# Cross-attention on one core: a new order table, scores with single banks, exponentials emitted bank by bank

## The chip, the core and the metric

The kernel runs on one core of a Trainium2 chip, in one launch. All data is fp32. The metric is the device time of that core in microseconds (us). Before the change the median of three runs is 495.86 us (495.84 to 495.98).

## The reference: what is computed

Tokens x (2 batches of 2048, width 640) attend to a context of 154 rows (width 1024) in 20 heads of 32. The first 77 context rows are text, the other 77 image prompts; each set has its own keys, values and softmax, and the two results are added. An output projection with bias follows, and x is added as residual:

```
q = heads(x @ Wq.T)
out = softmax(q k_text.T / sqrt(32)) v_text + softmax(q k_ip.T / sqrt(32)) v_ip
y = merge(out) @ Wo.T + bo + x
```

## The kernel before

Matrices come laid out with the contracted dimension first. The 640 channels are 5 chunks c of 128 (4 heads each), and a product q = 5 b + c names batch and chunk (0 to 9). Its 2048 tokens are two units u = 2 q and 2 q + 1 of 1024 tokens, each in two blocks h of 512. The 8 row tiles (128 tokens) of a unit fall into three groups s: 3, 3 and 2 tiles. Names are made of these numbers: `R1.12` is group 1 of unit 12.

For each group the work is a chain over four engines:

- `q.u.h` (line 206): TensorE projects 512 tokens into one PSUM bank, ten matmuls in the profile (each program matmul stands there as two). `cq` (line 220) is its scaled copy by ACT.
- `R` (line 242): scores of 4 heads, on 32-row tiles of the array, into four banks, one for each head. A group has 12 or 8 program matmuls (24 or 16 in the profile).
- `K` (line 254): ACT copies the four banks to `pb` in SBUF. `M` (line 290): VectorE takes maxima. `S` (line 304): POOL subtracts them. `E` (line 310): ACT's exponential. `D` (line 315): VectorE's sums; `I` (line 320): their reciprocals. `N` (line 325): POOL multiplies. `T` (line 332): VectorE transposes.
- Three sets name the groups that go another way. `DIRECT`: no K and no S; maxima are read out of the banks (line 293), and the exponential reads the banks with the maximum as bias, one activation for every row set of 77 (line 278). `BIASED`: K as usual, no S, the same small activations out of `pb`. `SUMMED`: the small activations also accumulate the sums, each with a read of the accumulator, and D falls away.
- `A.q` (line 341): the attention product of two units, 160 matmuls on 32x32 tiles, into four banks; `CA` (lines 364, 368) copies them out. It needs every `T` of both units, and the squares of v that `VS` (line 160) moves by 16 small transfers.

`k` and `v` (line 144) project the context, `ck` and `cv` copy it out. `m`, `o`, `p`, `z` (lines 480, 499, 509) are output products; batch 0 uses seven instead of eight products on halves, with sums `G` (POOL) of rows and `W` of weights and results taken by `cm` and `co` (VectorE). Batch 1 uses a scheme of 33 products `F` (line 887), with weight sums `V` (lines 864, 866) and sums of attention rows `X` (line 872), taken by `Y` (lines 827, 830). `X.B.p` is the first of these row sums; `.d` is VectorE and `.p` POOL.

Transfers go through SyncE's queue: `LK` loads weights of k and v, `LQ` of q, `LX` blocks of x for batch 1, `LO` the output weight, `SF` the residual, and `SS` stores.

What sets the order is a hand-fed table: `SCHEDULE` is one string of words, and `emit` issues each word's instructions. Every engine, and SyncE's queue, runs its own instructions strictly in the order of the table; waits come from the data, the buffers and the banks. `@` names the bank, or for R and A the half of PSUM: banks 0 to 3 or 4 to 7. In the rows of the order below, bank_67 to bank_74 are banks 0 to 7. Ahead of the table stands a fixed opening (the first projections and loads), which the change leaves as it is.

Of the kernel before, what the change touches and what calls it, by code (L numbers as in the profile page):

```python
# [9 lines left out]
F32 = mybir.dt.float32  # L10
AF = mybir.ActivationFunctionType
# [9 lines left out]
def kernel(  # L21
# [43 lines left out]
        (11, 0), (12, 0), (13, 0), (13, 2), (14, 0), (14, 2), (15, 1), (15, 2), (18, 1), (19, 2),  # L65
    }
    BIASED = {
        (2, 2), (3, 2), (4, 2), (6, 2), (8, 2), (9, 2), (11, 2), (12, 1), (16, 2), (17, 2), (18, 2),
    }
    SUMMED = {  # L70
        (4, 2), (11, 2), (12, 0), (13, 0), (13, 2), (14, 0), (15, 1), (15, 2), (16, 2), (17, 2), (18, 1),
        (18, 2), (19, 2),
# [13 lines left out]
    halves = banks[:G], banks[G:]  # L86
# [145 lines left out]
    def rows_of(u, s):  # L232
        return keys_of(u, s).rearrange("p n g (t l) -> p (n g) t l", l=L)
# [36 lines left out]
    def exponential_of(u, s, ps=None, den=None):  # L270

        n = GROUPS[s][1]
        for g in range(G):
            for t in range(n):
                for x in range(2):
                    row = rows_of(u, s)[:, t * G + g, x]
                    one = t * G + g, slice(x, x + 1)
                    nc.scalar.activation(  # L278
                        row,
                        row if ps is None else rows_in(ps[g], n)[:, t, x],  # L280
                        AF.Exp,
                        bias=maxs[(u, s)][:, *one],
                        accum_out=None if den is None else den[:, *one],
                    )
# [300 lines left out]
    for t in range(2):  # L585

        ps = halves[t][G - 2 + t]
        project_kv(t, ps)
        for b in range(B):
            nc.scalar.copy(kT[:, 0, b, t, :], keys_in(ps)[:, b])  # L590
# [345 lines left out]
```

## Time and profile before

| what | value |
|---|---|
| median of the runs | 495.86 us |
| span of the profiled execution | 494.6 us |
| TensorE busy | 489.1 us, 99% |
| VectorE busy | 413.9 us, 84% |
| POOL busy | 370.5 us, 75% |
| ACT busy | 309.5 us, 63% |
| granted TensorE clock | 1.00 throughout |
| HBM read and written | 54.94 and 10.49 MB |

The profile is of one execution; its own time is the span, from the first to the last instruction, and the median of the runs is 1.3 us above it. The chain of waits is followed back from the last instruction and lists each stretch with start, length, engine and line; the groups list busy time and mean length for each line and form; the timeline has the instructions in order of time with the idle time before them and what ended it. Matmul ends are modelled, so the distance from one start to the next says more than a matmul's own length.

### The profile page before, as it was taken

To read this page: it belongs to the slowest core of one execution; us is meant where nothing else is said; L and a number is where in the kernel's file an instruction comes from. 1 tells how busy PE (TensorE), PEld (TensorE's weight loads), DVE (VectorE), ACT (ScalarE), POOL (GpSimd) and SP (SyncE) were. 2 spreads that over 40 slices of the span, in tenths; PEclk is the share of its full clock that TensorE was granted. 3 is DMA by queue.
4 is the path that set the end of the run, shared out by engine and by line. 5 is a ranking of instruction groups with operands and counts; after the bars stand their busy time and mean duration, and the time that the engine had idled before them with its cause. 6 is when DMAs were issued, how large, how long until landed. Compare 5 with 4: busy or idle time off the path is not lost.

```text
span 494.6 us, 10484 instructions
## 1 busy us (share of the span) xinstructions
PE 489.1 (99%) x4116; PEld 287.7 (58%) x4116; DVE 413.9 (84%) x416; ACT 309.5 (63%) x1002; POOL 370.5 (75%) x158
## 2 busy tenths in 40 slices
PE   9999999999999999999999999999999999999997
PEld 5666648558557556456566654754755675444443
DVE  0069989989899989979988896687789898999996
ACT  1275788977687778677899786587889862100000
POOL 0069988988988988879886758475689899798700
PEclk9999999999999999999999999999999999999999
DMA  8992046203241724895540666455550212320125
GB/s 278 350 288 80 17 124 181 67 1 95 62 150 44 247 65 146 270 345 178 161 172 27 215 195 223 134 172 183 184 169 19 90 42 85 129 85 2 42 85 212
DMA packets 67105, 69.38 MB, mean 140 GB/s; under 512 B 5488, under 2 KB 47088, under 8 KB 67056
## 3 DMA queue, kind: packets, MB, share of 16 engines
q1 hardware_dynamic: 66048, 67.54, 43.7%
q10 hardware_dynamic: 1008, 1.18, 0.7%
q8 instruction: 32, 0.52, 0.4%
q14 instruction: 17, 0.14, 0.1%
HBM read 54.94 MB, written 10.49 MB: 132 GB/s over the span
## 4 chain that ended last, share of the span: by engine, by line
PE 96%; DMA 3%; ACTq 0%; ACT 0%; DVE 0%; DVEq 0%; issue 0%
PE bank L206 34%; PE bank L887 12%; PE bank L341 11%; PE bank L242 11%; PE bank L499 10%; PE bank L144 9%; PE bank L480 7%; PE bank L509 3%; DMA aT<-in_L_xattn_Wk_ip_dram 2%; DMA x<-in_x_dram 1%; ACTq L538 0%; ACT pb L254 0%; ACTq L552 0%; DVE acc L830 0%; DVEq L931 0%
## 5 line engine op out<-in xcount | busy, mean ns | idle before, releaser
L325 POOL TENSOR_TENSOR pb<-pb,rden 128x1848 f32<-128x1848 f32 (+1 forms) x60 | 176.0, 2943 | 30.4 <-DVE rden L320 23.6
L304 POOL TENSOR_TENSOR pb<-pb,mx 128x1848 f32<-128x1848 f32 (+1 forms) x39 | 121.6, 3129 | 55.4 <-DVE mx L290 55.3
L206 PE MATMUL bank<-x,wq 128*128 128x512 f32 x280 | 125.4, 598 | 0.1
L332 DVE STREAM_TRANSPOSE pb<-pb 128x1920 f32<-128x1920 f32 (+1 forms) x60 | 115.9, 1938 | 9.1 <-POOL pb L325 8.9
L290 DVE TENSOR_REDUCE mx<-pb 128x24 f32<-128x1848 f32 (+1 forms) x50 | 91.6, 1844 | 32.1 <-ACT pb L254 31.9
L254 ACT COPY pb<-bank 128x462 f32<-128x462 f32 (+1 forms) x200 | 85.3, 542 | 29.3 <-PE bank L242 28.9
L315 DVE TENSOR_REDUCE den<-pb 128x24 f32<-128x1848 f32 (+1 forms) x47 | 88.9, 1895 | 15.6 <-ACT pb L310 12.8
L206 PEld LDWEIGHTS bank<-x,wq 128*128 128x128 f32 x280 | 51.7, 190 | 60.0 <-issue 58.8
L310 ACT ACTIVATE pb<-pb 128x1848 f32<-128x1848 f32 (+1 forms) x39 | 65.6, 1684 | 17.5 <-POOL pb L304 17.4
L278 ACT ACTIVATE pb<-bank,mx 128x77 f32<-128x77 f32 x208 | 60.4, 387 | 6.5 <-DVE mx L293 6.5
L278 ACT ACTIVATE pb<-pb,mx 128x77 f32<-128x77 f32 x184 | 54.1, 356 | 1.9 <-DVE mx L290 1.8
L341 PE MATMUL bank<-pb,v 32*32 32x512 f32 x1600 | 55.2, 597 | 0.0
L206 PE MATMUL bank<-x,aT 128*128 128x512 f32 x116 | 51.8, 596 | 0.0
L242 PEld LDWEIGHTS bank<-kT,qT 32*128 32x128 f32 x1024 | 36.1, 184 | 21.6 <-issue 13.3
L144 PE MATMUL bank<-wo_ct,aT 128*128 128x154 f32 x320 | 46.0, 297 | 0.7 <-DMA aT<-in_L_xattn_Wk_ip_dram 0.4
L144 PEld LDWEIGHTS bank<-wo_ct,aT 128*128 128x128 f32 x320 | 43.0, 188 | 4.7 <-issue 3.0
L242 PE MATMUL bank<-kT,qT 32*128 32x154 f32 x1024 | 45.1, 305 | 0.0
L278 ACT ACTIVATION_READ_ACCUMULATOR pb<-bank,mx 128x1 f32 x168 | 44.0, 266 | 0.0
L341 PEld LDWEIGHTS bank<-pb,v 32*32 32x32 f32 x1600 | 29.0, 103 | 22.7 <-issue 10.1
L480 PE MATMUL bank<-aT,wo_ct 128*128 128x512 f32 x80 | 36.3, 595 | 0.0
L206 PEld LDWEIGHTS bank<-x,aT 128*128 128x128 f32 x116 | 21.4, 190 | 23.7 <-issue 23.5
L220 ACT ACTIVATE qT<-bank 128x512 f32<-128x512 f32 x32 | 19.3, 631 | 23.4 <-PE bank L206 23.4
(83 smaller groups left out, 524.2 us busy)
## 6 DMA issues: line engine op xcount, KB each, us to landing
x<-in_x_dram SPq DMA_DIRECT2D x20, 1280.0 KB, 6.7
out_dram<-acc SPq DMA_DIRECT2D x19, 256.0 KB, 2.9
x<-in_x_dram SPq DMA_DIRECT2D x17, 256.0 KB, 5.9
acc<-in_x_dram SPq DMA_DIRECT2D x16, 256.0 KB, 4.4
out_dram<-x SPq DMA_DIRECT2D x15, 256.0 KB, 2.0
v<-vS SPq DMA_DIRECT2D x160, 20.0 KB, 2.7
aT<-in_L_xattn_Wk_dram SPq DMA_DIRECT2D x5, 512.0 KB, 6.0
aT<-in_L_xattn_Wk_ip_dram SPq DMA_DIRECT2D x5, 512.0 KB, 5.5
```

The costliest lines, as they stand in the source:

```text
L144: nc.tensor.matmul(keys_in(out), loaded[n][:, k, :], cT[:, k, :, t, :], start=(k == 0), stop=(k == NCC - 1))
L206: nc.tensor.matmul(pq, weight_of(q)[:, k, :], xs[place_of(u, h)][:, k, :], start=(k == 0), stop=(k == NC - 1), skip_group_check=loose,)
L242: nc.tensor.matmul(ps[g][:, ts(t, 2 * L)], qTs[(u, h)][g * D : (g + 1) * D, ts(st, P)], kT[g * D : (g + 1) * D, c, b].rearrange("p t l -> ...
L254: nc.scalar.copy(keys_of(u, s)[:, :, g], ps[g][:, : n * 2 * L].rearrange("p (n l) -> p n l", n=n))
L278: nc.scalar.activation(row, row if ps is None else rows_in(ps[g], n)[:, t, x], AF.Exp, bias=maxs[(u, s)][:, *one], accum_out=None if den i ...
L290: nc.vector.tensor_reduce(mx, rows_of(u, s), AX.X, ALU.max, negate=negate)
L304: nc.gpsimd.tensor_tensor(rows_of(u, s), rows_of(u, s), maxs[(u, s)].unsqueeze(3).to_broadcast([P, n, 2, L]), ALU.subtract)
L315: nc.vector.tensor_reduce(den_of(u, s), rows_of(u, s), AX.X, ALU.add)
L325: nc.gpsimd.tensor_tensor(rows_of(u, s), rows_of(u, s), rdens[(u, s)].unsqueeze(3).to_broadcast([P, n, 2, L]), ALU.mult)
L332: nc.vector.transpose(p, p)
L341: nc.tensor.matmul(pa[r][g * D : (g + 1) * D, :], v4s[q % 2][rows, g, k, :], zones[rows, :, g, k, :], start=(k == 0), stop=(k == NK - 1),)
L480: nc.tensor.matmul(ps, wo[:, k, ts(NC - 1, P)], rows_of_attention(b, k)[:, i], start=(k == 0), stop=(k == NC - 1),)
```

## The change

1. The table has new words from its start up to the first sum of attention rows (`X.B.p`); behind it the words are nearly the same, with a few neighbours swapped and other bank numbers.
2. R and A no longer take a half of PSUM. The table names four banks, in the order in which the four heads (for A the four row groups) use them.
3. The exponential of a small-activation group is emitted in four words, one for each bank: `E0.1.0` to `E0.1.3`. A group with one big activation still runs it at the first of the four; the other three do nothing.
4. The three sets change: 10 to 8 groups DIRECT, 11 to 13 BIASED, 13 to 16 SUMMED.

The computation is otherwise the same. The diff, with two lines of the table for many:

```diff
     DIRECT = {
-        (11, 0), (12, 0), (13, 0), (13, 2), (14, 0), (14, 2), (15, 1), (15, 2), (18, 1), (19, 2),
+        (1, 2), (9, 1), (11, 0), (13, 0), (13, 2), (15, 1), (18, 1), (19, 2),
     }
     BIASED = {
-        (2, 2), (3, 2), (4, 2), (6, 2), (8, 2), (9, 2), (11, 2), (12, 1), (16, 2), (17, 2), (18, 2),
+        (2, 2), (4, 2), (5, 2), (6, 2), (8, 2), (11, 2), (12, 1), (13, 1), (15, 2), (16, 2), (17, 2), (18, 2),
+        (19, 1),
     }
     SUMMED = {
-        (4, 2), (11, 2), (12, 0), (13, 0), (13, 2), (14, 0), (15, 1), (15, 2), (16, 2), (17, 2), (18, 1),
-        (18, 2), (19, 2),
+        (1, 2), (2, 2), (4, 2), (5, 2), (6, 2), (8, 2), (11, 2), (12, 1), (13, 1), (15, 1), (15, 2), (16, 2),
+        (17, 2), (18, 1), (18, 2), (19, 2),
     }
...
-    halves = banks[:G], banks[G:]
...
-    def exponential_of(u, s, ps=None, den=None):
+    def exponential_of(u, s, g, ps=None, den=None):
         n = GROUPS[s][1]
-        for g in range(G):
-            for t in range(n):
-                for x in range(2):
+        for t in range(n):
+            for x in range(2):
...
-        "A.4@1 K1.10 M2.10 S0.10 M1.10 S2.10 E0.10 q.12.1@1 CA.4 D0.10 S1.10 E2.10 D2.10 R0.11@1 cq.12.1 E1.10 "
...
+        "K0.10 q.12.0@2 T2.9 T1.9 G5.0 LX.12.1 LX.13.0 VS.5.1 cq.12.0 R1.10@1460 M2.10 K1.10 A.4@3752 M0.10 S2.10 "
+        "M1.10 R0.11@1460 CA.4 q.12.1@3 M0.11 W0 S0.10 E2.10.0 LQ.7 E0.11.0 LX.14.0 VS.6.0 E0.11.1 W1 m2.0@2 "
...
         if k[0] == "R":
-            at[name] = halves[int(where)]
+            at[name] = [banks[int(n)] for n in where]
             scores(x, i, at[name])
         elif k == "A":
-            at[name] = halves[int(where)]
+            at[name] = [banks[int(n)] for n in where]
             attend(x, at[name])
...
                 elif direct or biased:
-                    exponential_of(
-                        x, i, ps if direct else None, den_of(x, i) if (x, i) in SUMMED else None
-                    )
-                else:
+                    if (x, i) in SUMMED and (x, i) not in dens:
+                        den_of(x, i)
+                    exponential_of(x, i, int(args[1]), ps if direct else None, dens.get((x, i)))
+                elif args[1] == "0":
                     exponential(x, i)
```

The places that the prediction speaks of follow, as rows of one engine in program order (line, operation, what it writes and reads, size; line numbers of the changed kernel are one lower from the output sums on). A line of dots leaves out rows of the same run.

TensorE at unit 4, groups 2 and 0 (R2.4 and R0.4) behind the projection q.5.0, before:

```order
L206 MATMUL bank_73<-x_84,aT 128x512 x5
L242 MATMUL bank_67<-kT,aT 128x154
...
L242 MATMUL bank_70<-kT,aT 128x154
L242 MATMUL bank_71<-kT,aT 128x154
L242 MATMUL bank_72<-kT,aT 128x154
L242 MATMUL bank_73<-kT,aT 128x154
...
L144 MATMUL bank_67<-wo_ct,aT 128x154 x8
```

And now:

```order
L206 MATMUL bank_69<-x_84,aT 128x512 x5
L242 MATMUL bank_70<-kT,aT 128x154
...
L242 MATMUL bank_68<-kT,aT 128x154
L144 MATMUL bank_72<-wo_ct,aT 128x154 x8
L242 MATMUL bank_69<-kT,aT 128x154
...
L242 MATMUL bank_72<-kT,aT 128x154
L206 MATMUL bank_69<-x_85,aT 128x512 x5
```

Before, the second group's third bank (73) is the one that the projection had just written; now its bank (69) comes first in a run that the context projection v.2.0 (L144) precedes, and groups 0 and 1 of unit 4 follow each other.

TensorE at unit 12, before (R1.12, q.13.0, the output product m1.0, R0.12):

```order
L242 MATMUL bank_67<-kT,qT_1_1957 128x154
...
L242 MATMUL bank_70<-kT,qT_1_1957 128x154
L206 MATMUL bank_74<-x_82,wq_75 128x512 x5
L499 MATMUL bank_73<-aT,wo_ct 128x256 x4
L242 MATMUL bank_67<-kT,qT_0_1827 128x154
...
L242 MATMUL bank_70<-kT,qT_0_1827 128x154
L206 MATMUL bank_72<-x_83,wq_76 128x512 x5
```

And now (o.0, R0.12, R1.12, m1.0, q.13.0):

```order
L479 MATMUL bank_68<-aT,wo_ct 128x512 x5
L242 MATMUL bank_74<-kT,qT_0_1838 128x154
...
L242 MATMUL bank_68<-kT,qT_1_2004 128x154
L498 MATMUL bank_74<-aT,wo_ct 128x256 x4
L206 MATMUL bank_69<-x_82,wq_75 128x512 x5
```

The two score groups of unit 12 were parted by a projection and an output product; now they are one run, and its last bank (68) is the one that o.0 wrote just ahead of it.

SyncE's queue around the output weight (L166), ahead of A.4, before:

```order
L160 DMA v_0_80<-vS_0_93 32x160 x8
L468 DMA res<-in_x_dram 128x512
L188 DMA x_83<-in_x_dram 128x5x512
L194 DMA wq_75<-in_L_xattn_Wq_dram 128x5x128
L160 DMA v_0_80<-vS_0_93 32x160 x8
L188 DMA x_84<-in_x_dram 128x5x512
L166 DMA wo_ct<-in_L_xattn_Wo_dram 128x5x640
```

And now:

```order
L160 DMA v_0_80<-vS_0_93 32x160 x8
L194 DMA wq_75<-in_L_xattn_Wq_dram 128x5x128
L188 DMA x_83<-in_x_dram 128x5x512
L166 DMA wo_ct<-in_L_xattn_Wo_dram 128x5x640
L160 DMA v_0_80<-vS_0_93 32x160 x8
L188 DMA x_84<-in_x_dram 128x5x512
```

The output weight moved ahead of the last eight v transfers (VS.4.1) and of the block for q.12.1 (x_84); the fetch into `res` moved far ahead.

More of the change, by code (lines that the diff above doesn't have):

```diff
@@ L268, in den_of @@
         return dens[(u, s)]
-    def exponential_of(u, s, ps=None, den=None):
+    def exponential_of(u, s, g, ps=None, den=None):
         n = GROUPS[s][1]
-        for g in range(G):
-            for t in range(n):
-                for x in range(2):
[L276 to L283, printed above, removed]
-                    )
+        for t in range(n):
+            for x in range(2):
+                row = rows_of(u, s)[:, t * G + g, x]
+                one = t * G + g, slice(x, x + 1)
+                nc.scalar.activation(
+                    row,
+                    row if ps is None else rows_in(ps[g], n)[:, t, x],
+                    AF.Exp,
+                    bias=maxs[(u, s)][:, *one],
+                    accum_out=None if den is None else den[:, *one],
+                )
     def maxima(u, s, ps=None, negate=False):
@@ L585 @@
     for t in range(2):
-        ps = halves[t][G - 2 + t]
+        ps = banks[G * t + G - 2 + t]
         project_kv(t, ps)
@@ L701, in emit @@
                 elif direct or biased:
-                    exponential_of(
-                        x, i, ps if direct else None, den_of(x, i) if (x, i) in SUMMED else None
-                    )
-                else:
+                    if (x, i) in SUMMED and (x, i) not in dens:
+                        den_of(x, i)
+                    exponential_of(x, i, int(args[1]), ps if direct else None, dens.get((x, i)))
+                elif args[1] == "0":
                     exponential(x, i)
```

140 rows, old and new, of the table SCHEDULE are left out of this document.

## The prediction, on record before the result

> **What bounds the kernel now.** I read the page first, then the chain of waits in order of time, then busy time by stretch, then groups by form. From the page, the span, the busy time of each engine, the granted clock and the make-up of the chain that ended last:
>
> ```profile
> span 494.6 us, 10484 instructions
> PE 489.1 (99%) x4116; PEld 287.7 (58%) x4116; DVE 413.9 (84%) x416; ACT 309.5 (63%) x1002; POOL 370.5 (75%) x158
> PEclk9999999999999999999999999999999999999999
> PE 96%; DMA 3%; ACTq 0%; ACT 0%; DVE 0%; DVEq 0%; issue 0%
> ```
>
> TensorE is busy 99% of the span at full clock, and 96% of the last chain is TensorE. So an order can win only what TensorE loses between pieces of work. A busy share does not show this, because matmul ends are modelled; the chain does. Its rows are start, length, engine and line, matmuls joined (each program matmul stands as two):
>
> ```profile
> 39.38 1.78 PE bank L242 x48
> 96.01 4.29 PE bank L206 x10
> 100.30 1.00 PE bank L242 x24
> 101.30 4.49 PE bank L206 x10
> 105.79 5.45 PE bank L341 x154
> 111.24 1.00 PE bank L242 x24
> 116.65 1.52 PE bank L242 x40
> ```
>
> L242 is a score run (word R), L206 a projection of queries (q), L341 an attention product (A). First, score runs of 24, 40 and 48 matmuls take 1.00, 1.52 and 1.78: 0.0325 per matmul and 0.22 for the run however long it is, also right behind an A (111.24). Two R words back to back pay the 0.22 once. Second, the same ten matmuls of L206 take 4.29 behind another full-array piece and 4.49 behind R: coming back from the small tiles of R or A to the full array costs 0.20. I call R and A words with nothing else between them a tile stretch.
>
> Third, real waits. A pair of R words (x40) should take 1.52. In this fence stand all the pairs that took longer, with what followed where the wait spilled over:
>
> ```profile
> 91.96 1.74 PE bank L242 x38
> 129.06 1.74 PE bank L242 x38
> 166.16 1.75 PE bank L242 x40
> 203.34 1.03 PE bank L242 x24
> 204.38 0.53 ACT pb L254
> 204.95 4.56 PE bank L206 x10
> 228.53 1.67 PE bank L242 x39
> 273.35 1.76 PE bank L242 x40
> ```
>
> The excess is 0.22, 0.22, 0.23, 0.16 (203.34 to 204.95 is 1.61, or 0.09, and 4.56 against 4.49 another 0.07), 0.18 (228.53 to the next piece at 230.23 is 1.70) and 0.24: 1.25 us together. All have one cause: the pair needs the banks of one half in fixed order, and one of them was written 0.6 to 1.0 us before by a q, o or m word that ACT or DVE has not yet read out.
>
> **The change part by part.**
>
> *Form changes.* Read off the TensorE words of the two tables, the tile stretches ahead of and with A.9 fall from 50 to 46 and the score runs in them from 46 to 44. Up to A.4 both counts are equal (22 and 22 ahead of it); the gain lies between A.4 and A.9. Saved: 4 x 0.20 + 2 x 0.22 = 1.24 us. TensorE's work itself is the same, matmul for matmul, so nothing else changes in its sum.
>
> The Trainium skill's page "TensorE: Matmul & The Clock Gate", section "Part 3: Packing small matmuls — row/col tiling", says that weight loads overlap running matmuls only when the row groups differ. By it full-array loads would lie open everywhere, the return from tiles would cost nothing extra, and this term would be 0.44. The rows disagree: the return costs 0.20 in each row shown. I go by the rows.
>
> *Bank waits.* Every R and A word now names its four banks one by one. The bank freed last is put last in its run, or a short projection stands between. Where the order shows q.5.0 on bank 69, v.2.0 now stands between the two score words and R0.4 has 2.9 us instead of 0.69 until it needs that bank, so the 0.22 at 91.96 is gone; likewise at 129.06. In other places the bank need stays short. By the words and the lengths above: R0.8 needs the bank of q.9.0, and R0.10 that of q.11.0, 0.72 us after it (0.69 cost 0.22 before, so about 0.19 each). o.0 and o.1 take the first bank of an R word with only one short R (0.63 us) between. Such a first copy ends some 0.8 us after its run: 0.17 each. R1.12 needs o.0's bank and R2.11 that of m2.0 0.98 us after them, as the rows at 228.53 and 273.35 did (0.18 and 0.24) where VectorE reads the bank; it may be free in time, so I take half, 0.10 each. Sum 0.92, from 0 (all hidden) to 1.25 (no better than before). Saved: 1.25 - 0.92 = 0.33.
>
> *Work on the other engines.* The three sets that choose how a group of attention rows is computed change. Forms and mean lengths in ns, from the groups by form:
>
> ```profile
> L315 DVE TENSOR_REDUCE den<-pb 128x16 f32<-128x1232 f32 x12 | 17.0, 1416 | 3.8 <-ACT pb L310 2.2 <-ACT pb L278 1.5
> L290 DVE TENSOR_REDUCE mx<-pb 128x16 f32<-128x1232 f32 x16 | 22.5, 1409 | 2.8 <-ACT pb L254 2.6
> L293 DVE TENSOR_REDUCE mx<-bank 128x4 f32<-128x308 f32 x16 | 6.5, 469 | 1.1 <-PE bank L242 1.1
> L304 POOL TENSOR_TENSOR pb<-pb,mx 128x1848 f32<-128x1848 f32 x33 | 108.3, 3289 | 54.5 <-DVE mx L290 54.5
> L278 ACT ACTIVATION_READ_ACCUMULATOR pb<-pb,mx 128x1 f32 x80 | 16.1, 202 | 0.0
> ```
>
> Ahead of A.4, five more small groups sum on ACT: VectorE loses 5 x 1.42 = 7.1 us of sums and gains under 1 us for two groups that reduce out of banks (four of 0.47 for one of 1.41 in the small one). ACT pays 5 x 16 accumulator reads of 0.20 = 16 us at most; they partly run under the next activation, so 8 to 16. POOL does one subtraction of 3.29 less. How much room there is:
>
> ```profile
> 27.00:210.00 183.00, 182.91 (x1793) 112.23 (x1795) 170.51 (x129) 139.41 (x324) 163.24 (x55) 1.00 0.42 120
> 140.22 2.17 DVE L332 STREAM_TRANSPOSE pb<-pb 128x1920 f32<-128x1920 f32 x1
> 142.88 5.45 PE bank L341 x150
> ```
>
> The first row (27 to 210 us) has TensorE, weight loads, DVE, ACT and POOL. VectorE is busy 170.5 of 183, and its last transpose for A.2 ends at 142.39, 0.49 ahead of A.2. So VectorE is the engine that could stop TensorE, and the change takes 6 us from it just there; ACT goes from 139 to at most 155 of 183. All this is hidden beside TensorE and I cost it at 0. Without that cover, a late transpose is paid one to one at the next A. A summed group is now emitted a bank at a time, in four pieces, so that copies on ACT's queue, and then TensorE, wait behind 4 or 6 activations at most, not 16 or 24.
>
> *The tail.* From the first sum of rows on, order and work are nearly the same. It must start earlier, or it swallows the gain. The links closest to TensorE:
>
> ```profile
> 417.77 2.18 DVE L332 STREAM_TRANSPOSE pb<-pb 128x1920 f32<-128x1920 f32 x1 [0.36 <-POOL pb L325]
> 427.41 1.48 DVE L872 TENSOR_TENSOR pb<-aT 128x1024 f32<-128x1024 f32 x1 [0.36 <-PE bank L341]
> 440.60 1.37 POOL L866 TENSOR_TENSOR pb<-wo_ct,pb 128x128 f32<-128x128 f32 x1 [1.19 <-DVE pb L866]
> 441.93 0.45 POOL L866 TENSOR_TENSOR pb<-pb,wo_ct 128x128 f32<-128x128 f32 x1
> 442.85 1.88 PE L887 MATMUL bank<-aT,pb 128*128 128x512 f32 x4
> ```
>
> The weight sum that ends at 442.38 is used at 442.85, 0.47 later. Its chain starts behind A.9 with VectorE's row sum at 427.41, ahead of which VectorE idles 0.36. It moves with A.9 if the last transpose (417.77) is earlier too. That hangs on POOL, which drops the subtraction of unit 19's middle group, 3.29 us, just there. So I cost the tail at 0; bounds 0 and 0.8 (below).
>
> Sum: 1.24 + 0.33 = 1.57 us. The profiled span is 494.6 and the median 495.86, so 1.3 us lie around the span and stay. 495.86 - 1.57 = **494.3 us**. A measurement here tells a change from none at about 0.2%, or 1.0 us.
>
> **The rivals.**
>
> *Swallowed (chance 0.22).* If the last transpose does not move, the row sum at 427.41 starts only 0.36 earlier and the use at 442.85 can come 0.36 + 0.47 = 0.83 earlier: 495.0, no change to be told. New waits of 0.6 to 2.5 us at other short leads end in the same place. For it: VectorE's lead of 0.49 at A.2 shows how tightly one engine follows another. Against it: the 3.29 less on POOL.
>
> *Transfers ahead of A.4 (chance 0.15), slower.* SyncE now issues the whole output weight between a block of x and the last eight v transfers that A.4 needs:
>
> ```profile
> 196.18 0.38 SPq L188 DMA_DIRECT2D x<-in_x_dram  x1
> 197.17 7.21 SPq L160 DMA_DIRECT2D v<-vS  x8
> 204.48 0.53 SPq L188 DMA_DIRECT2D x<-in_x_dram  x1
> 205.05 0.52 SPq L166 DMA_DIRECT2D wo_ct<-in_L_xattn_Wo_dram  x1
> DMA to landing us min/median/max: 9.6/9.6/9.6
> DMA to landing us min/median/max: 6.1/6.7/13.6
> DMA to landing us min/median/max: 1.7/2.7/13.2
> ```
>
> The landing rows are of the output weight, the x blocks and the v transfers. Issued 0.57 behind a block that took the least, 6.1, the weight landed 214.65 - 210.58 = 4.1 later. Eight issues took 7.21 us where the first took about 0.6, so the late ones wait for earlier landings. Now: block issued near 196, as before, and landed near 202.7, weight near 206.8, last v 1.7 to 2.7 later, at 208.5 to 209.5. A.4 is due near 209.7 (210.51 before, less the 0.83 of waits ahead of it). It holds by 0.2 to 1.2 us. If the weight lands more than 1 us later, A.4 waits one to one, and behind the v transfers stands the block for q.12.1, due at 216. It decides the sign from about 2.6 us of wait; with 3 us: 494.3 + 3 = 497.3. For it: a v transfer has taken 13.2 us behind such blocks. Against it: one small fetch (the 0.26 MB into `res`) leaves this place. The Trainium skill's page "DMA: Bandwidth & Descriptors", section "Two DMAs through the same engine are not ordered", says that descriptors in one queue start in order; the 13.2 agrees.
>
> *By the skill's rule on weight loads (0.03).* Returns cost nothing, so 495.86 - 0.44 - 0.33 = 495.1, no change.
>
> *The table does not do what it says (0.02).* Waits return elsewhere for each one removed: 495.9. The order shows otherwise.
>
> **How the numbers follow.** The forecast, 494.3, has 0.58, with its own range 493.3 (1.24 and all 1.25 of waits saved, 495.86 - 2.49) to 494.8. Faster is 0.58; the same 0.22 + 0.03 + 0.02 = 0.27; slower 0.15. The range for 8 in 10 reaches over the no-change cases to just past their edge: 493.3 to 496.1.
>
> **What would show it.** In the new chain: 46 stretches, R1.12 as part of one 1.78 run with R0.12, A.4 followed at once by a run of 24; x40 pairs near 1.52 at q.5.0 and q.7.0; A.9 starting 1.3 to 2 us before 421.8; 442.85 moved as far as A.9. Wrong, if TensorE stands ahead of A.4 on a v transfer, if A waits for a transpose, or if A.9 comes early and the matmul at 442.85 does not.

## The result and the profile after

The changed kernel takes 502.77 us (median of 499.7 to 504.22) against 495.92 us for the kernel before (495.7 to 496.92). By the medians it is slower by 6.85 us, where 1.57 us faster was forecast. The ratio on record is 1.0125, with a 95% interval of 1.0103 to 1.0148, which is 5.1 to 7.3 us. Two things need explaining: the profiled execution is only 3.3 us longer than that of before (span 497.9 against 494.6), and the executions of the changed kernel lie 4.5 us apart.

From the page of the changed kernel, the span, the busy time of the engines and the make-up of the last chain:

```profile
span 497.9 us, 10506 instructions
PE 488.2 (98%) x4116; PEld 288.3 (58%) x4116; DVE 412.1 (83%) x407; ACT 317.8 (64%) x1058; POOL 368.7 (74%) x158
PE 66%; DVE 13%; POOL 9%; ACT 6%; DMA 3%; issue 1%; SPq 0%; ACTq 0%; DVEq 0%; POOLq 0%
```

TensorE was 96% of the last chain before; now it is 66%. The other engines stand in the chain where they did not. The share overstates it: another trace of the same kernel, 0.5 us shorter, has 84%, for a chain goes over to whatever engine was last, by however little. How much time that costs is read from the attention products, A.4, A.7, A.8 and A.9, in the chain of waits (start, length, engine and line). Before:

```profile
210.51 5.45 PE bank L341 x150
344.81 5.46 PE bank L341 x150
387.23 5.48 PE bank L341 x151
421.87 5.45 PE bank L341 x150
```

And of the changed kernel, with three score runs (L242) between them:

```profile
209.92 5.52 PE bank L340 x149
223.52 1.82 PE bank L242 x40
229.83 2.02 PE bank L242 x48
272.54 1.84 PE bank L242 x40
343.71 5.45 PE bank L340 x149
388.04 5.45 PE bank L340 x154
424.90 5.51 PE bank L340 x150
```

At A.7 the changed kernel is 1.1 us ahead, at A.8 it is 0.8 behind, at A.9 3.0 behind. Of the 1.1 only 0.5 were won between A.0 and A.7; the rest stands ahead of A.0. The two stretches behind A.7 cost 4.1 us, and 3.0 of it is left at A.9. By the first matmul of each A (the chain's rows start up to 0.07 later), in us; the third column, the kernel with both waits mended, comes from an experiment below:

| stretch | before | changed | both mended |
|---|---|---|---|
| start to A.0 | 68.62 | 68.00 | 68.60 |
| A.0 to A.4 | 141.82 | 141.92 | 141.91 |
| A.4 to A.7 | 134.30 | 133.72 | 133.67 |
| A.7 to A.8 | 42.42 | 44.33 | 42.28 |
| A.8 to A.9 | 34.64 | 36.86 | 34.62 |
| A.9 to the end | 72.77 | 73.08 | 73.14 |

The first row hangs on the first loads; with the changed kernel's opening it lies between 67.6 and 69.6 from trace to trace (68.6 and 69.5 also occur with the old table), and is no effect of the change. TensorE's waits, as the profile groups them, name the two places:

```profile
PE bank L498 <- DVE acc L529: 2.0, 1, 2.0
PE bank L206 <- DMA x<-in_x_dram: 1.9, 1, 1.9
```

**The first is a transfer.** The projection q.19.1 (L206) waits for its block of x. The end of the chain that leads to it:

```profile
357.63 3.29 DMA out_dram<-acc
360.93 0.37 SPq L469
361.35 6.99 DMA x<-in_x_dram
368.48 4.53 PE bank L206 x10
```

The block (LX.19.1) is issued at 361.35 and lands 6.99 later. It stands on SyncE's queue behind a fetch into `acc` (SF.3.0, L469), which may not start before the store out of the same place (SS.2.0) has landed, at 360.92. Further ahead stands the run of eight v transfers VS.9.0. SyncE's queue there:

```profile
348.32 0.46 SPq L188 DMA_DIRECT2D x<-in_x_dram  x1
348.88 8.03 SPq L160 DMA_DIRECT2D v<-vS  x8
```

Eight issues took 8.03 us; the last waited for the landing of the block issued at 348.32, eight issues ahead of it. Before, q.19.1 came behind q.19.0, and its rows on SyncE's queue and in the chain were:

```profile
364.26 0.46 SPq L188 DMA_DIRECT2D x<-in_x_dram  x1
...
375.86 4.49 PE bank L206 x10
```

The change puts q.19.1 ahead of q.19.0, so it is due at 366.6, more than 9 us earlier, while its load is issued only 2.9 us earlier.

**The second is a collision of VectorE with POOL.** VectorE's timeline in the changed kernel (L319 is the reciprocal I1.19, L880 the weight sum V.Q.0.d, L882 V.P.1.d, L529 the read-out cm6.3 that frees the bank), and POOL's beside it (L882 the sums V.E.0.p and V.D.0.p, L324 the multiplication N1.19):

```profile
408.86 0.29 DVE L319 RECIPROCAL rden<-den 128x24 f32<-128x24 f32 x1
409.07 0.23 DVE L882 TENSOR_TENSOR pb<-pb,wo_ct 128x128 f32<-128x128 f32 x1
409.33 3.40 DVE L880 SCALAR_TENSOR_TENSOR pb<-pb,wo_ct 128x128 f32<-128x128 f32 x1
412.66 0.67 DVE L529 TENSOR_TENSOR acc<-acc,bank 128x512 f32<-128x512 f32 x1
```

```profile
406.77 0.86 POOL L882 TENSOR_TENSOR pb<-wo_ct 128x128 f32<-128x128 f32 x2
409.30 3.29 POOL L324 TENSOR_TENSOR pb<-pb,rden 128x1848 f32<-128x1848 f32 x1 [1.67 <-DVE pb L882]
```

The same in the kernel before, VectorE and then POOL:

```profile
408.45 0.22 DVE L866 TENSOR_TENSOR pb<-pb,wo_ct 128x128 f32<-128x128 f32 x1
408.70 0.42 DVE L864 SCALAR_TENSOR_TENSOR pb<-pb,wo_ct 128x128 f32<-128x128 f32 x1
```

```profile
407.97 1.01 POOL L866 TENSOR_TENSOR pb<-wo_ct 128x128 f32<-128x128 f32 x2
408.94 5.54 POOL L325 TENSOR_TENSOR pb<-pb,rden 128x1848 f32<-128x1848 f32 x2
```

The same sum of 128 by 128 took 0.42 us before and 3.40 now; it ended 0.14 after POOL's multiplication, which had begun 0.03 ahead of it. The multiplication needs the reciprocal I1.19 and began 0.14 after its end (409.16); elsewhere in this trace, where POOL was idle and waited for a reciprocal, the distance is mostly the same 0.14. So the profile's name for what POOL waited for, V.P.1.d, which ended at the same moment, says little. Before, POOL was still at its own sums and began the multiplication at 408.94, when V.Q.0.d was already running. So the two engines seem to shut each other out of something that both need, and I call it a port; the rows show the exclusion, not the part. Behind V.Q.0.d stands cm6.3, and TensorE's m7.3 needs the bank that cm6.3 reads.

The traces give these two as candidates. The experiments test whether they are the loss, and where the rest comes from, since 1.9 and 2.0 us do not make 6.85.

### The profile page after: what moved, and what is told of

Read it like the earlier page. It is cut to its first block, busy times and chain, and to the rows that moved or that the text cites. A ratio compares the mean times of both kernels' runs of the same rounds, so it can differ in the third digit from the quotient of the medians.

```text
span 497.9 us, 10506 instructions
## 1 busy us (share of the span) xinstructions
PE 488.2 (98%) x4116; PEld 288.3 (58%) x4116; DVE 412.1 (83%) x407; ACT 317.8 (64%) x1058; POOL 368.7 (74%) x158
## 4 chain that ended last, share of the span: by engine, by line
PE 66%; DVE 13%; POOL 9%; ACT 6%; DMA 3%; issue 1%; SPq 0%; ACTq 0%; DVEq 0%; POOLq 0%
PE bank L206 20%; PE bank L903 11%; PE bank L498 10%; PE bank L340 8%; PE bank L242 7%; PE bank L479 5%; POOL pb L303 5%; POOL pb L324 4%; PE bank L144 4%; DVE pb L331 4%; DVE mx L289 3%; DVE den L314 3%; PE bank L508 3%; ACT pb L277 2%; ACT pb L309 2%; DMA x<-in_x_dram 1%
## 5 line engine op out<-in xcount | busy, mean ns | idle before, releaser
L324 POOL TENSOR_TENSOR pb<-pb,rden 128x1848 f32<-128x1848 f32 (+1 forms) x60 | 175.5, 2942 | 43.7 <-DVE rden L319 40.2
L206 PE MATMUL bank<-x,wq 128*128 128x512 f32 x280 | 124.4, 596 | 1.9 <-DMA x<-in_x_dram 1.9
L289 DVE TENSOR_REDUCE mx<-pb 128x24 f32<-128x1848 f32 (+1 forms) x52 | 95.0, 1844 | 35.9 <-ACT pb L254 35.8
L331 DVE STREAM_TRANSPOSE pb<-pb 128x1920 f32<-128x1920 f32 (+1 forms) x60 | 114.7, 1926 | 3.2 <-POOL pb L324 2.9
L254 ACT COPY pb<-bank 128x462 f32<-128x462 f32 (+1 forms) x208 | 88.6, 535 | 21.5 <-PE bank L242 21.3
L314 DVE TENSOR_REDUCE den<-pb 128x24 f32<-128x1848 f32 (+1 forms) x44 | 85.0, 1942 | 11.0 <-ACT pb L309 10.1
L206 PEld LDWEIGHTS bank<-x,wq 128*128 128x128 f32 x280 | 52.2, 190 | 62.4 <-issue 58.4
L277 ACT ACTIVATE pb<-pb,mx 128x77 f32<-128x77 f32 x232 | 78.1, 377 | 3.5 <-DVE mx L289 3.5
L309 ACT ACTIVATE pb<-pb 128x1848 f32<-128x1848 f32 (+1 forms) x39 | 64.6, 1667 | 22.8 <-POOL pb L303 22.7
L206 PE MATMUL bank<-x,aT 128*128 128x512 f32 x116 | 51.9, 598 | 0.7 <-DMA aT<-in_L_xattn_Wq_dram 0.7
L242 PEld LDWEIGHTS bank<-kT,qT 32*128 32x128 f32 x1024 | 36.5, 184 | 19.9 <-issue 15.6
L277 ACT ACTIVATE pb<-bank,mx 128x77 f32<-128x77 f32 x168 | 44.4, 380 | 4.1 <-DVE mx L292 4.0
L277 ACT ACTIVATION_READ_ACCUMULATOR pb<-pb,mx 128x1 f32 x208 | 46.1, 221 | 0.0
L144 PE MATMUL bank<-wo_ct,aT 128*128 128x154 f32 x320 | 45.6, 296 | 0.2 <-ACT aT L367 0.2
L242 PE MATMUL bank<-kT,qT 32*128 32x154 f32 x1024 | 44.9, 305 | 0.2 <-ACT qT L220 0.2
L144 PEld LDWEIGHTS bank<-wo_ct,aT 128*128 128x128 f32 x320 | 42.9, 188 | 3.6 <-issue 2.2
L206 PEld LDWEIGHTS bank<-x,aT 128*128 128x128 f32 x116 | 21.3, 190 | 25.5 <-issue 24.9
L498 PE MATMUL bank<-aT,wo_ct 128*128 128x256 f32 x128 | 32.7, 388 | 2.0 <-DVE acc L529 2.0
```

The lines of the kernel that those rows point to most:

```text
L144: nc.tensor.matmul(keys_in(out), loaded[n][:, k, :], cT[:, k, :, t, :], start=(k == 0), stop=(k == NCC - 1))
L206: nc.tensor.matmul(pq, weight_of(q)[:, k, :], xs[place_of(u, h)][:, k, :], start=(k == 0), stop=(k == NC - 1), skip_group_check=loose,)
L242: nc.tensor.matmul(ps[g][:, ts(t, 2 * L)], qTs[(u, h)][g * D : (g + 1) * D, ts(st, P)], kT[g * D : (g + 1) * D, c, b].rearrange("p t l -> ...
L254: nc.scalar.copy(keys_of(u, s)[:, :, g], ps[g][:, : n * 2 * L].rearrange("p (n l) -> p n l", n=n))
L277: nc.scalar.activation(row, row if ps is None else rows_in(ps[g], n)[:, t, x], AF.Exp, bias=maxs[(u, s)][:, *one], accum_out=None if den i ...
L289: nc.vector.tensor_reduce(mx, rows_of(u, s), AX.X, ALU.max, negate=negate)
```

## The experiments

### The changed kernel again

No edit.

> The changed kernel itself once more, because its six times lie between 499.7 and 504.2 us while its profiled execution, the fastest of them, has a span of 497.9. Theory 1: two waits make the loss, the projection q.19.1 waiting 1.9 us for its block of x and the output product behind p.0 waiting 2.0 us for VectorE's weight sum V.Q.0.d, which ran 3.40 us instead of 0.42 because POOL's multiplication began 0.03 us before it; the slower executions then show the same two places, the first one longer. Theory 2: the cover that VectorE gave to TensorE is gone (its last transpose ended only 0.06 to 0.4 us ahead of A.2, A.4, A.5, A.6 and A.8) and slower executions show transposes late at these A. Expected median 501 to 504; a span above 500 tells the theories apart by where the additional time stands.

Measured: 501.45 us (499.27 to 504.1), ratio 1.0105 (1.0059 to 1.0152). The profiled execution again shows the two waits, 2.0 and 1.4 us, in the same places. It is one of the shorter ones, so where the longer ones lose more stayed open.

### The block of x issued earlier

```diff
-  E1.16.2 SF.2.2 M2.17 SS.2.0 ... cm5.2 SF.3.0 ... G4.2 LX.19.1 M1.17 VS.9.1
+  E1.16.2 LX.19.1 SF.2.2 M2.17 SS.2.0 ... cm5.2 SF.3.0 ... G4.2 M1.17 VS.9.1
```

> Only the load of the last block of x (LX.19.1) moves on SyncE's queue, ahead of SF.2.2, SS.2.0 and SF.3.0, so that it is issued near 357.0 us instead of 361.35 and lands near 364, 2.5 us before q.19.1 is due. Theory 1: the wait of 1.9 us in the profiled execution is gone, and if it is also what makes the other executions longer (up to 4.5 us more), the median falls by 2 to 6 us, to 497 to 501. Theory 2 (late transposes): the median falls by 2 us at most and the times still spread by 4 us.

Measured: 498.82 us (497.47 to 499.9), ratio 1.0052 (1.0036 to 1.0068), 2.6 us below the changed kernel beside it. The wait for the block is gone; the one on the port stays at 2.0. The block is issued at 357.92, directly behind VS.9.0, though this execution reached A.0 0.8 us later. More seems won than the 1.9 us that the trace has as a wait, but the interval of the changed kernel beside it is some 2 us wide to either side.

### VectorE's two sums ahead of the reciprocal

```diff
-  p.0@2 cm3.3 I1.19 V.P.1.d V.Q.0.d N1.19 cm6.3
+  p.0@2 cm3.3 V.P.1.d V.Q.0.d I1.19 N1.19 cm6.3
```

> Only VectorE's order changes: the weight sums V.P.1.d and V.Q.0.d stand ahead of the reciprocal I1.19, so POOL's multiplication N1.19, which needs that reciprocal, cannot begin before V.Q.0.d has begun. Theory 1: V.Q.0.d takes 0.4 us again, the wait of 2.0 us behind p.0 goes, and the median falls by 2.0 us, less some tenths for N1.19 starting 0.4 us later: 500.5 to 501. Rival: V.Q.0.d is long for its operands or its place in the table and not for POOL; then it still takes 3.4 us and nothing is won.

Measured: 499.0 us (497.69 to 500.31), ratio 1.0058 (1.0036 to 1.008), 2.45 below the changed kernel and so more than was expected. VectorE's and POOL's timelines:

```profile
410.57 0.28 DVE L882 TENSOR_TENSOR pb<-pb,wo_ct 128x128 f32<-128x128 f32 x1
410.88 0.29 DVE L880 SCALAR_TENSOR_TENSOR pb<-pb,wo_ct 128x128 f32<-128x128 f32 x1
411.09 0.30 DVE L319 RECIPROCAL rden<-den 128x24 f32<-128x24 f32 x1
```

```profile
411.53 3.29 POOL L324 TENSOR_TENSOR pb<-pb,rden 128x1848 f32<-128x1848 f32 x1 [2.19 <-DVE rden L319]
```

V.Q.0.d takes 0.29 us where POOL cannot be reading, and POOL begins 0.14 behind the reciprocal here too; A.8 to A.9 is 34.61 us again. The rival, that its operands or place make it long, falls.

### Both

> Both edits together. Theory 1: the span of the profiled execution is 497.9 - 1.9 - 2.0 = 494.0, and the median 495.0 to 497 if the two waits are also what differs between executions. If late transposes or another wait make the rest, the median stays at 498 or above with the profiled execution well below it.

Measured: 496.16 us (494.92 to 497.12), ratio 1.0003 (0.9989 to 1.0016): as fast as the kernel before, and the spread is 2.2 us, near the 2.0 of the kernel before beside it. These two small edits of the table take back 5.3 us. Alone the two edits gave 2.6 and 2.45. Against the mean of all eleven executions of the changed kernel (502.0, on three occasions) the means of the three kernels give 3.3, 3.0 and 5.9. So the two waits make the loss, and nearly add up; and each seems worth more than its 1.9 or 2.0, as if something were paid behind a wait.

### A longer execution of the changed kernel

No edit.

> The changed kernel once more, for the trace of one of its longer executions (six of ten so far had spans of 500.3 to 502.4 us at a mean granted clock of 0.996 to 0.993, four had 497.4 to 498.2 at 0.999 to 1.000). Theory of the clock: in a longer execution the two waits of about 2 us are there as before, and behind one or both of them the granted clock falls for a few us; a mean of 0.9965 is one stretch of 3.4 us at half clock in 497, 0.993 two of them, and each costs about 1.7 us. Rival: the waits themselves are longer (the block of x lands up to 5 us later), and the lower mean only counts idle time. A span of 498 or less would tell nothing new.

Measured: 502.81 us; the span is 501.0 and the mean granted clock 0.997. Busy time by stretch of 1 us, with the granted clock in the third column from the end (then the share of the DMA engines, and GB/s), and TensorE's row for q.19.1:

```profile
371.00:372.00 1.00, 1.00 (x3) 0.36 (x2) 1.00 (x1) 0.62 (x4) 1.00 (x1) 0.63 0.08 19
372.00:373.00 1.00, 1.00 (x3) 0.35 (x2) 1.00 (x2) 0.00 (x0) 1.00 (x1) 0.50 0.01 1
...
374.00:375.00 1.00, 1.00 (x3) 0.36 (x2) 0.56 (x1) 0.00 (x0) 1.00 (x1) 0.67 0.00 0
```

```profile
369.91 6.23 PE L206 MATMUL bank<-x,wq 128*128 128x512 f32 x10 [2.24 <-DMA x<-in_x_dram]
```

The wait is 2.24 us, hardly longer than in the shorter execution. But 1.3 us after TensorE is back at work its clock halves, for 3.4 us (half clock in 0.74 of the stretch at 371, all of the next two, 0.66 of the last), and the ten matmuls take 6.23 us instead of 4.53. Half of 3.4 is 1.7, and 1.7 is the difference. The rival, that the block lands much later, falls. Of the 3.1 us that this execution is longer, 2.1 stand between A.7 and A.8; the other 1.1 stand ahead of A.0. The spans of all executions of this order go with their mean clock: four at 0.999 to 1.000 lie at 497.9 on average, three at 0.996 to 0.997 at 500.8, four at 0.993 at 502.0. One stretch of 3.4 us at half clock is 0.0034 of the mean, so these are none, one and two stretches, about 2 us apiece on average (2.9 and 1.2, with starts that differ by up to 2 us). A mean of 0.996 or 0.997 also stands in some executions of each kernel with one mend, but in none with both. So either wait can bring such a stretch. That both did in one execution is inferred from 0.993; no trace has it.

Whether a wait brings one can be read from the traces. In all of them the granted clock changes only at steps of 3.413 us: between a trace's first rise to full clock and its last change, every stretch at one clock is a whole number of them (1 and 2 at half clock, 106, 37, 143 and others at full). Cut into these steps, this execution has TensorE idle for 2.07 us in the step ahead of the fall. The steps at full clock in the thirteen traces of this study, up to the last matmul, by TensorE's idle time in them:

| idle in a step of 3.413 us | steps | clock in the next step |
|---|---|---|
| 2.00 to 3.41 us | 6 | half, each time |
| 0 to 1.93 us | 1840 | full, each time |

The shorter executions fit: in the changed kernel's first trace the wait of 1.9 us was divided into 0.57 and 1.31 between two steps, and the wait of 2.0 us put 1.93 into one. So a wait of about 2 us is paid twice only where it falls almost whole into one step. The idle times are as exact as the modelled matmul ends.

### The block of x issued later

On the kernel with VectorE's sums mended:

```diff
-  LX.19.1 M1.17 VS.9.1
+  M1.17 VS.9.1 LX.19.1
```

> The kernel with VectorE's weight sums mended, and the load of the last block of x (LX.19.1) moved the other way, behind the eight v transfers VS.9.1, so that TensorE waits for it some 6 to 9 us instead of 1.9. Theory of the clock: after this wait TensorE's granted clock falls in the profile to about half for some us, projections take up to 0.86 us a matmul instead of 0.43 there, and the span grows by the wait plus 1.7 to 3.4 us, to 503 to 509. Rival: the clock stays at 1.00 after the wait and the span grows by the longer wait alone.

Measured: 505.02 us, span 503.2, mean clock 0.993. TensorE's row, and two of the stretches:

```profile
373.74 6.82 PE L206 MATMUL bank<-x,wq 128*128 128x512 f32 x10 [6.79 <-DMA x<-in_x_dram]
```

```profile
373.00:374.00 1.00, 0.26 (x1) 0.29 (x2) 0.85 (x1) 0.00 (x0) 1.00 (x1) 0.50 0.02 6
378.00:379.00 1.00, 1.00 (x3) 0.49 (x2) 0.00 (x0) 0.00 (x0) 0.00 (x0) 0.82 0.00 0
```

The clock is down before the block lands and stays at half until 378.4, 4.6 us into the projection; the ten matmuls lose 6.82 - 4.53 = 2.3 us. This wait of TensorE is paid twice: as it stands, and in the clock behind it.

### Five sums given back to VectorE

On the kernel with both mends:

```diff
     SUMMED = {
-        (1, 2), (2, 2), (4, 2), (5, 2), (6, 2), (8, 2), (11, 2), ...
+        (4, 2), (11, 2), ...
-  I2.1 ... I2.2 ... I2.5 ... I2.6 ... I2.8
+  D2.1 I2.1 ... D2.2 I2.2 ... D2.5 I2.5 ... D2.6 I2.6 ... D2.8 I2.8
```

> Both mends, and of the three sets the part ahead of A.4 undone: the small groups of units 1, 2, 5, 6 and 8 are summed by VectorE again (five sums of 1.42 us), not by ACT's accumulator. The prediction's step says that these sums were hidden, so that taking them from VectorE is worth nothing by itself. If that is so, the median stays within 0.5 us of 496.2. Rival: VectorE's transposes set the start of A.2 and A.4 now (0.10 and 0.06 us ahead in the trace), and each sum put back delays them one to one: A.2 by up to 1.4, A.4 by up to 1.4 more, the median at 497.5 to 499.

Measured: 500.85 us (500.75 to 501.46), ratio 1.0095 (1.0078 to 1.0112), 4.7 us above both mends (496.16, measured on another occasion). That is beyond the rival's 497.5 to 499 too. A.0 to A.1 grows by 1.3 us, A.1 to A.2 by 2.7, and A.2 to A.4 by 0.85, 4.85 together. At A.2, VectorE and TensorE:

```profile
142.71 3.56 DVE L331 STREAM_TRANSPOSE pb<-pb 128x1920 f32<-128x1920 f32 x2
```

```profile
146.37 2.20 PE L340 MATMUL bank<-pb,v 32*32 32x512 f32 x56 [1.57 <-issue]
```

The last transpose ends at 146.27 and A.2 starts at 146.37, after 1.57 us of idle time. A.1 waits in the same way, for 0.34. The larger part, some 2.7 us, TensorE waits at four places for copies by ACT (L363, L367, L734). All four stand on ACT behind an exponential that waited for a subtraction by POOL, and in three of them POOL had waited for VectorE's maxima: VectorE again, by a longer way. The mean clock is 1.000 in all four executions; TensorE waits much in all, but for 1.57 us at most at one place of the profiled one. In the changed kernel itself the transposes come as late, at A.2 and at A.4:

```profile
138.18 3.56 DVE L331 STREAM_TRANSPOSE pb<-pb 128x1920 f32<-128x1920 f32 x2
...
204.14 5.73 DVE L331 STREAM_TRANSPOSE pb<-pb 128x1920 f32<-128x1920 f32 x3
```

They end at 141.74 and 209.87; the A start at 141.84 and 209.92. Before the change the leads were 0.43 (0.49 in the prediction, by the chain's row) and 0.35. The 0.10 and 0.05 are no lead at all: A.2 stood 0.10 behind its transpose where it waited 1.57 us for it. The new order has spent what the sets freed: five sums of 1.42 us, 7.1 together, come back as 4.7. What the sets alone would do in the old order was not tried.

### The exponentials in one piece

On the kernel with both mends:

```diff
-  E0.0.0 E0.0.1 E0.0.2 v.0.0@6 E1.0.0 E1.0.1 cv.0.0 E1.0.2 E0.0.3 E1.0.3
+  E0.0.0 E0.0.1 E0.0.2 E0.0.3 v.0.0@6 E1.0.0 E1.0.1 E1.0.2 E1.0.3 cv.0.0
   (and so for every group)
```

> Both mends, and the emission bank by bank undone: the four pieces of each exponential follow each other at the place of the first, as before the change. The prediction costed the pieces at 0 as a cover for copies on ACT's queue. If they are not needed, the median stays at 496.2. If they are, a copy of scores or queries now stands behind up to 24 activations of 0.38 us (9 us at most) in this order, TensorE waits for banks at several places, and the median rises by 3 us or more.

Measured: 533.27 us, ratio 1.0745 (1.0718 to 1.0773), 37 us slower. TensorE's largest waits are three of 7.8 us together for copies of scores by ACT (L254). A place in the chain:

```profile
83.42 5.43 ACT pb L277 x32
88.84 0.18 ACT kT L731
...
89.07 1.90 PE bank L242 x18
```

A copy of keys (L731) stands behind a whole group of small activations, and the scores wait for it. The pieces are no spare cover: this order is built on them. Not all of the 37 us are waits: the profiled execution is at half clock for 17 us ahead of its end, which is up to 8.5 us of it.

### The port in the kernel before

Two edits of the kernel before, each POOL's two sums alone, first a little earlier, then behind the multiplication:

```diff
-  D1.19 p.0@4 cm3.3 I1.19 V.E.0.p V.P.1.d V.D.0.p V.Q.0.d N1.19 E0.19
+  V.E.0.p V.D.0.p D1.19 p.0@4 cm3.3 I1.19 V.P.1.d V.Q.0.d N1.19 E0.19
```

> The kernel before, with one thing of the change alone: POOL's weight sums V.E.0.p and V.D.0.p stand a little earlier, ahead of D1.19, as in the changed table. POOL is then free when the reciprocal I1.19 is done and its multiplication N1.19 starts about 0.03 us before VectorE's V.Q.0.d (408.68 against 408.70), where before it waited for V.D.0.p until 408.94. Theory of the shared port: V.Q.0.d then takes about 3.4 us instead of 0.42, TensorE waits some 2 us for the bank that cm6.3 reads out, and the median rises by 2.0 to 2.6 us, to 498 to 498.9. Rival (something else of the new order makes V.Q.0.d long): nothing changes, 495.5 to 496.5. If V.Q.0.d still comes first by a hair, the theory gives no change either; the trace tells by its start.

Measured: 496.31 us, ratio 1.0002 (0.9991 to 1.0013). It tells nothing on the port, for the edit did not reach the place. POOL's timeline:

```profile
405.64 3.28 POOL L304 TENSOR_TENSOR pb<-pb,mx 128x1848 f32<-128x1848 f32 x1
```

POOL is busy with a subtraction until 408.92 in this execution (which reached A.0 0.9 us later), so its sums, which stand behind that in either order, cannot start earlier. The words moved only past words of other engines, and no engine's own order changed.

```diff
-  I1.19 V.E.0.p V.P.1.d V.D.0.p V.Q.0.d N1.19 E0.19
+  I1.19 V.P.1.d V.Q.0.d N1.19 V.E.0.p V.D.0.p E0.19
```

> The kernel before, with POOL's weight sums V.E.0.p and V.D.0.p moved behind the multiplication N1.19, so that POOL has nothing between its subtraction S0.19 (done at 408.0) and N1.19 and waits for the reciprocal, as in the changed kernel. Neither sum is needed by V.Q.0.d. Theory of the shared port, in the form the traces of the changed kernel give it (N1.19 began at 409.30, the moment V.P.1.d ended): N1.19 starts when V.P.1.d ends, ahead of V.Q.0.d, which then takes 3.3 to 3.5 us; TensorE waits about 2 us ahead of m7.3, and the median rises by 2.0 to 3.2 us, to 498.1 to 499.3. Rival: V.Q.0.d was long for another reason, it takes 0.42 us here, and the median stays at 495.7 to 496.5.

Measured: 499.16 us (498.45 to 499.58), ratio 1.0068 (1.0049 to 1.0086). VectorE and POOL:

```profile
408.26 0.29 DVE L320 RECIPROCAL rden<-den 128x24 f32<-128x24 f32 x1
408.73 3.40 DVE L864 SCALAR_TENSOR_TENSOR pb<-pb,wo_ct 128x128 f32<-128x128 f32 x1
```

```profile
408.70 3.29 POOL L325 TENSOR_TENSOR pb<-pb,rden 128x1848 f32<-128x1848 f32 x1 [0.66 <-DVE pb L866]
```

V.Q.0.d is 3.40 us long again, in the old table, and A.8 to A.9 grows by 2.35 us. Nothing else of the new order is needed for it: it is enough that POOL is free when the reciprocal comes. Its multiplication then begins 0.14 behind the reciprocal, which is 0.03 ahead of V.Q.0.d.

### Two small waits more

On the kernel with both mends: ACT's copies swapped, and banks 4 and 7 exchanged in four products F.

```diff
-  cq.11.1 N2.9 D1.9 cq.10.1 cq.11.0 R2.10@2375
+  cq.10.1 cq.11.1 N2.9 D1.9 cq.11.0 R2.10@2375
...
-  F25.1@7 ... F26.0@4 ... F4.0@4 ... F22.1@7
+  F25.1@4 ... F26.0@7 ... F4.0@7 ... F22.1@4
```

> Both mends, and two small waits more that its trace still shows: ACT copies q.10.1 ahead of q.11.1, since R2.10 stood 0.25 us at 203.4 for that copy, and banks 4 and 7 change places among the last products F, since F25.1 stood 0.30 us at 435.5 for a bank that VectorE read. Sum 0.55 us. The accounting by intervals gives a span 0.5 us below that of the two mends, and a median of 495.5 to 495.8; it cannot be told from the kernel before (495.8 to 496.4 in these comparisons) unless the ratio is below 0.998. If the waits only move to the transposes at A.4 (0.06 us ahead), 0.3 of it stays.

Measured: 495.85 us (495.0 to 496.96), ratio 0.9992 (0.9983 to 1.0001). A.9 to the end is 72.73 instead of 73.14, so the exchange of banks gave its 0.3 to 0.4. The swap of copies gave nothing: A.3 to A.4 stays at 33.1, for the wait moved from the three projections ahead of R2.10 (13.32 to 13.07 us) into the score pair behind them (1.52 to 1.76). From A.0 to the end this kernel takes 425.4 us and the one before 425.95. It is the best order of this study and not faster than the kernel before by more than the measurement is uncertain.

## Why the prediction was wrong, step by step

**The bound** was read right for the kernel before and assumed for the new one. With 96% of the old chain on TensorE, an order can win what TensorE loses between pieces; but the new order was allowed to lose elsewhere.

**Form changes, forecast 1.24 us: right.** From A.0 to A.9 the traces hold the same matmuls in both orders, in 43 tile stretches before and 39 now, with 40 and 38 score runs: 4 x 0.20 + 2 x 0.22 = 1.24 us. With the prediction's lengths, and 0.216 a matmul for the output products, A.6 to A.9 comes out to within 0.1 us in the kernel with both mends, so these lengths hold in the new order. A run of 24 follows A.4, as said, and R0.12 and R1.12 are one run of 48.

**Bank waits, forecast 0.33 saved: wrong sign, small.** A.0 to A.9 is 0.70 us shorter with both mends (352.47 against 353.17) where the pieces give 1.24, so 0.55 more is left beside them than before. Between A.0 and A.2 0.35 is saved, of the forecast's 0.44 for the two pairs there; between A.3 and A.4 0.47 is lost, where the run R0.9 behind A.3 takes 1.27 instead of 1.00 and the projections ahead of R2.10 wait 0.25 for a copy. The pair with R2.11 takes 1.82 instead of 1.52, the run with R1.12 2.02 instead of 1.78, where 0.10 each was taken, and the pair with R2.13 (1.84 at 272.54) was not in the list. A lead worked out from the order says nothing of whether the engine that frees the bank is free itself; which of these waits came from that was not tried.

**Work on the other engines, forecast 0: the step gave VectorE's gain away as surplus.** Its bookkeeping held: from 27 to 210 us VectorE is busy for 163.7 us instead of 170.5, and ACT for 145.2 instead of 139.4, less than the 147 to 155 of the estimate. It said that 7.1 us of sums less on VectorE are hidden. They are not: the new order uses them up, and without them it is 4.7 us slower. Of the pieces of the exponential it said only that they shorten a queue on ACT; they are worth up to 37 us to this order. The total of the step, nothing, happens to be near, because both were in place. It was the wrong question: not what the parts save, but how much lead is left behind them. At A.2 and A.4 it fell from 0.43 and 0.35 us to the 0.10 and 0.05 of a TensorE that waits.

**The transfers ahead of A.4, the slower rival at 0.15: right mechanism, wrong place.** Its arithmetic held. SyncE's queue in the changed kernel, the output weight and the eight v transfers:

```profile
195.85 0.52 SPq L166 DMA_DIRECT2D wo_ct<-in_L_xattn_Wo_dram  x1
196.41 10.89 SPq L160 DMA_DIRECT2D v<-vS  x8
```

The weight landed 10.9 us after its issue, at 206.8 as estimated, the last v transfer at 208.55 and A.4 started at 209.92. But the prediction followed SyncE's queue at one place only, the one where the words for transfers had visibly changed neighbours. The place that broke, q.19.1, came 9.3 us earlier on TensorE and its load 2.9 us on SyncE, behind a store's landing. This is the first step that failed: the sum put every transfer but those ahead of A.4 at nothing, without a reason. The block of x cost 2.05 us (A.7 to A.8), and 1.7 more where the clock fell behind the wait. For every piece that is moved ahead, the transfer it reads must be looked up, with what it stands behind.

**The tail, forecast 0 with bounds 0 and 0.8: the step that failed most in the table of stretches.** It said that from the first sum of rows on, order and work are nearly the same, and so cost nothing. Nearly the same words met in another relative time: POOL was free earlier, began its multiplication 0.03 us ahead of V.Q.0.d and kept the port for 3.29 us. That is 2.2 us, outside both bounds. The prediction had the row of the 3.29 us that POOL drops and counted it as a gain for the chain. The Trainium skill says on the page "SBUF — State Buffer", section "Who interferes with whom", that a VectorE instruction with two SBUF inputs contends with an instruction of GpSimd (POOL here) that reads SBUF, that the shared pair of ports is an exclusive lock, and that the order of issue decides who blocks. The rows of V.Q.0.d (0.42 and 0.29 us against 3.40, twice) agree; the rule spoke against the change and was not weighed. The kernel before shows the exclusion in its own rows. Of VectorE's sums of attention rows, the ones that begin at 430.06 take 4.76 us for two, where the one at 427.41 in the prediction takes 1.48:

```profile
428.92 1.22 DVE L872 TENSOR_TENSOR pb<-aT,pb 128x1024 f32<-128x1024 f32 x1
430.06 4.76 DVE L872 TENSOR_TENSOR pb<-aT 128x1024 f32<-128x1024 f32 x2
```

POOL had begun such a sum at 429.06, behind the start of VectorE's at 428.92; it took 3.28 us, where most of POOL's take 2.36. The rows fit an exclusion in which each engine in turn was held by the other, and a price for such a collision could be read there. The other 0.3 of the tail is F25.1, which was given a bank that VectorE still had to read.

**The sum.** For the profiled executions: -0.6 of the start, -1.25 of the forms, +0.55 of bank waits, +2.1 for the block of x, +2.2 for the port, +0.3 of the tail make +3.3, the difference of the spans. The medians are 6.85 apart: the profiled execution of the changed kernel, without a stretch of low clock, is 3.1 us under its median (499.7 against 502.77), and that of before 0.5 over its own. Behind the waits the runs show a clock at half speed for 3.4 us, none, one or two times in an execution. No rival of the prediction priced a wait above its length. The prediction gave slower a chance of 0.15, for a place that did not break. The lower end of the prediction's range, 495.86 - 2.49, is 493.4 and not 493.3, which changes nothing. Also, each execution's time is 1.8 us above its own span (499.7 and 497.9 for the profiled one); the 1.3 of the prediction set the span of one execution against the median of others.

## What to carry to other kernels

When an order is changed, look up for every piece that comes earlier the transfer and the read-out it needs, and where these stand in their own queues; the piece that moved without its load is the one that waits. Give a VectorE instruction that reads two operands from SBUF a place where POOL can't start a long one just ahead of it, for instance ahead of the value that POOL waits for. Count the lead that is left at each wait, not the busy time that is freed, and where TensorE is the bound count a wait of 2 us as up to 4 (2.24 and 1.7 in the longer execution here).

## What the runs showed of the hardware that was not expected

- A gap of 2.24 us in otherwise dense matmuls was enough to halve TensorE's clock for 3.4 us, beginning 1.3 us after work had resumed; of the eleven executions with two waits of about 2 us, seven show it in their mean clock and four do not. In all thirteen traces the clock fell behind every step of 3.413 us in which TensorE was idle for 2.00 us or more, and behind none with 1.93 or less. The Trainium skill, "TensorE: Matmul & The Clock Gate", section "What's actually happening", gives windows of about 3.4 us that run freely and an idle window as the condition. The length and the free running agree; that the whole window must be idle does not, since 2.00 us of it did.
- A start 0.03 us earlier decided 3 us: POOL's multiplication began 0.14 us behind the reciprocal it needs, V.Q.0.d 0.18 behind it, and V.Q.0.d took 3.40 us, in each of the traces with that order.
- Transfers behind each other on SyncE's queue were held by the landing of the one eight issues ahead: the eighth v transfer of VS.9.0 was issued at 356.40, when the block issued at 348.32 had landed at 356.34. None of the 296 issues in the traces of before, of the change and of both mends begins before the landing of the one eight ahead, and the closest come 0.02 behind it. Whether the chip or the program sets this was not tried.
